# Two chained layers on one core: where the projection is added to the input, and where the second layer is prepared

## The chip, the core and the metric

The kernel runs on one core of a Trainium2 chip, all in float32. The metric is the device time of one execution in microseconds (us). The engines are PE (matrix multiply), DVE (vector), ACT (activations, scalar engine), POOL (GpSimd) and SP, which here only issues DMAs; ACT and POOL issue DMAs too, each engine in the order of its own queue. [...]

## What is computed

The input x is 384 channels of 192 x 192. Two layers follow each other, each added to its input:

```python
# layer 0
n = group_norm(x)                          # 32 groups of 12 channels
qkv = max_pool_2x2(w_qkv @ n + b_qkv)      # 1152 channels, 96 x 96
qkv = depthwise_3x3(qkv) + b_dw
q, k, v = split(qkv)                       # 8 heads of 48 channels
s = (q / |q|) @ (k / |k|).T * temperature  # 48 x 48 per head
out = sum(a_i * softmax(keep_top(s, k_i)) @ v for 4 sizes k_i)
x = x + repeat_2x2(w_proj @ gelu(out) + b_proj)
# layer 1
n = group_norm(x)
x = x + sum(bn_i(depthwise(n, w_i)) for 7 kernels)   # 13x13 and six smaller, dilated ones
```

The seven depthwise convolutions of layer 1 are folded into one 13 x 13 kernel per channel; the residual is put into its middle tap, as 1/scale of the group norm.

## The kernel before

**First statistics (lines 141 to 206).** x is loaded once, DVE takes bn_stats, and `group_stats` (109) turns channel statistics into scale and shift per channel (`gn0`) through small matmuls with the group matrix. The tap images' zero gaps are written to DRAM (`zd`).

**qkv stage (218 to 411).** 24 blocks of 8 input rows. A block has 18 steps (9 output groups of 128 channels, two halves): PE projects (`project`), DVE takes the 2x2 maximum out of PSUM (`pool`, line 280), ACT adds the bias, and one or two steps later DVE adds eight depthwise taps, four per step (`taps`, 316). PSUM holds two projections. Queries and keys are transposed and multiplied into a Gram matrix. ACT normalizes the next block's input in steps 9 to 14. The order is written out by hand: `at(step, f)` puts a piece of work ahead of a later step.

**Attention (414 to 529).** Ranks, softmax and the four masks become one block-diagonal matrix `bd`.

**Projection stage (532 to 594).** 24 blocks of 4 rows of 96. PE multiplies `bd` with v ("av", line 556), ACT applies Gelu, PE multiplies with w_proj ("pj", 567), ACT adds the bias (571), DVE adds the result to two rows of a fresh copy of x (577) and takes its statistics (581), POOL stores the sum to DRAM as `x1d`, rows of four interleaved (584).

**Layer 1, preparation (599 to 684).** From the statistics follow scale and shift (`group_stats`, `chp`); 1/scale goes into the middle tap; DVE spreads each channel's taps into 32 shifted images (`z`, 648), which are written to `zd`; matmuls make the tables `cb` (from `sv`) and `par` (from `rep`, "pp") and `edge`.

**Layer 1, convolution (686 to 816).** 48 tiles of 8 channels, and in a tile 8 x 5 matmuls with the tap images as weights. For each tile SP loads rows (`raw`, four transfers of 32 partitions, u = 0 to 3) and taps (`wt`, the same), ACT normalizes (726), DVE arranges into 16-column patches (741), PE multiplies (756), ACT evicts (764) out of four PSUM buffers, DVE turns the result back (770) and POOL stores it (779). Rows are loaded three tiles ahead, taps two, normalize runs two ahead, arrange one.

Of the kernel before, what the change touches and what calls it, by code (L numbers as in the profile page):

```python
# [45 lines left out]
PROW = MR * W  # L46
# [16 lines left out]
def tile_attn_then_large_kernel_conv(ctx: ExitStack, tc: tile.TileContext, a: dict, out: bass.AP):  # L63
# [7 lines left out]
    x1d = dram.tile([UQ * C * PROW + 2 * W], F32, name="x1d")  # L71
    zd = dram.tile([C * 32 * ZR * BC + 7 * BC], F32, name="zd")

    def x1_at(u, c, m):
        return x1d.offset + W + (u * C + c) * PROW + m * W
# [33 lines left out]
    def group_stats(pool, psum, mv, name):  # L109

        ps = psum.tile([NG, 1], F32, tag="gs", name=f"{name}_ps")
# [3 lines left out]
        nc.vector.tensor_copy(mean, ps)  # L115

        s = pool.tile([P, NJ, 1], F32, name=f"{name}_s")
        for j in range(NJ):
            pb = psum.tile([P, 1], F32, tag="gs", name=f"{name}_pb{j}")
            nc.tensor.matmul(pb, lhsT=gmt[:, j * P : (j + 1) * P], rhs=mean, start=True, stop=True)  # L120
            nc.vector.tensor_sub(s[:, j], mv[:, j, 0:1], pb)
            nc.vector.scalar_tensor_tensor(s[:, j], s[:, j], s[:, j], mv[:, j, 1:2], ALU.mult, ALU.add)
# [9 lines left out]
        return sb  # L132


    gn0 = const.tile([P, NJ, 2], F32, name="gn0")
    with (
# [57 lines left out]
        zero = s1.tile([1, W], F32, name="zero")  # L194
        nc.gpsimd.memset(zero, 0.0)
        for o in (0, W + UQ * C * PROW):
            nc.gpsimd.dma_start(out=bass.AP(x1d.tensor, x1d.offset + o, [[W, 1], [1, W]]), in_=zero)

        mv0 = s1.tile([P, NJ, 2], F32, name="mv0")
        for j in range(NJ):  # L200
            nc.vector.bn_aggr(mv0[:, j, :], stats[:, j].rearrange("p n s -> p (n s)"))
        sb0 = group_stats(s1, s_ps, mv0, "g0")
        for j in range(NJ):
            pb = s_ps.tile([P, 2], F32, tag="gs", name=f"g0_pc{j}")
            nc.tensor.matmul(pb, lhsT=gmt[:, j * P : (j + 1) * P], rhs=sb0, start=True, stop=True)
            nc.vector.tensor_copy(gn0[:, j, :], pb)  # L206


    mv1 = const.tile([P, NJ, 2], F32, name="mv1")
    with ExitStack() as ctx_v:  # L210
# [7 lines left out]
        with tc.tile_pool(name="gram", bufs=1, space=PSUM) as gps:  # L218
            gram = gps.tile([2 * CH, NPR, 2 * CH], F32, name="gram")
            with (  # L220
# [4 lines left out]
                tc.tile_pool(name="trps", bufs=2, space=PSUM) as trps,  # L225
            ):
# [35 lines left out]

                def project(b, m, sb):
# [14 lines left out]
                def pool(b, m, sb, ps):  # L278
                    mx = aw.tile([P, SR, WS], F32, tag="mx", name="mx", bufs=3)
# [45 lines left out]
                def end(b, m):  # L325

                    if m < 2 * NJ:
                        na = rows(b)[2]
                        junk = aw.tile([P, R + 1, WS], F32, name=f"junk_{b}_{m}", tag="junk")
                        nc.scalar.activation(  # L330
                            junk[:, :na], accs[b, m][:, :na], AF.Square, accum_out=ssq[:, m, b : b + 1]
                        )
# [49 lines left out]
                with tc.manual_schedule():  # L382
# [3 lines left out]
                    for sb in range(2):  # L386
                        for j in range(NJ):
                            normalize(0, sb, j)
                    for s in range(NB * NU):
# [8 lines left out]
                        if 9 <= u < 15 and b + 1 < NB:  # L398
                            normalize(b + 1, *divmod(u - 9, NJ))
                        if sb == 1:  # L400
# [14 lines left out]
            late_pool = ctx_v.enter_context(tc.tile_pool(name="late", bufs=1))  # L415
            bd = late_pool.tile([P, NJ, C], F32, name="bd")
            stats1 = late_pool.tile([P, NJ, HW // 512, 6], F32, name="stats1")
# [115 lines left out]
        NBK = RB * WS  # L533
        with (
            tc.tile_pool(name="b1", bufs=1) as b1,
            tc.tile_pool(name="bx", bufs=3) as bx,
            tc.tile_pool(name="bw", bufs=2) as bw,
            tc.tile_pool(name="b_ps", bufs=3, space=PSUM) as b_ps,
        ):
            wp = b1.tile([P, NJ, C], F32, name="wp")  # L540
            nc.sync.dma_start(out=wp, in_=a["wprojT"].rearrange("(j p) o -> p j o", p=P))
            bpj = b1.tile([P, NJ], F32, name="bpj")
            nc.sync.dma_start(out=bpj, in_=a["b_proj"])
            for b in range(HS // RB):
                r0 = 2 * b * RB
                xt = bx.tile([P, NJ, 2 * RB, W], F32, tag="xt", name=f"xb_{b}")
                nc.sync.dma_start(
                    out=xt.rearrange("p j r w -> p j (r w)"),
                    in_=x[:, r0 * W : (r0 + 2 * RB) * W].rearrange("(j p) n -> p j n", p=P),
                )  # L550
                g = bw.tile([P, NJ, NBK], F32, tag="g", name=f"g_{b}")
                for i in range(NJ):
                    ps = b_ps.tile([P, NBK], F32, tag="av", name="av")
                    js = AV_BLOCKS[i]
                    for j in js:
                        nc.tensor.matmul(
                            ps,
                            lhsT=bd[:, j, i * P : (i + 1) * P],
                            rhs=v[:, j, b * RB : (b + 1) * RB, :].rearrange("p r w -> p (r w)"),
                            start=(j == js[0]),  # L560
                            stop=(j == js[-1]),
                        )
                    nc.scalar.activation(g[:, i, :], ps, AF.Gelu)  # L563
                for i in range(NJ):
                    ps = b_ps.tile([P, NBK], F32, tag="pj", name="pj")
                    for j in range(NJ):
                        nc.tensor.matmul(  # L567
# [298 lines left out]
```

## Time and profile before

| | us |
|---|---|
| median of 3 runs (3372.46 to 3374.98) | 3374.6 |
| the profiled execution | 3371.7 |
| its span, first to last instruction | 3370.0 |
| PE busy | 2988.8 |
| DVE busy | 2572.3 |
| ACT busy | 1057.4 |
| POOL busy | 248.6 |

The profile is of one execution. A line of its groups of instructions gives source line, engine, operation, output<-inputs, shapes and count, then busy time, mean ns of one, and the idle time of the engine just before these instructions with what ended it. A float32 matmul of the program appears as two instructions. In rows by stretch of time each engine has its busy time, followed by PE's granted clock (1.00 is full), the share of time in which the 16 DMA engines were busy, and GB/s. The chain of waits goes back from the last instruction to what released each step. A DMA line gives the KB of one transfer and the median time from issue to landing.

### The profile page before, as it was taken

To read this page: it belongs to the slowest core of one execution; us is meant where nothing else is said; L and a number is where in the kernel's file an instruction comes from. 1 tells how busy PE (TensorE), PEld (TensorE's weight loads), DVE (VectorE), ACT (ScalarE), POOL (GpSimd) and SP (SyncE) were. 2 spreads that over 40 slices of the span, in tenths; PEclk is the share of its full clock that TensorE was granted. 3 is DMA by queue.
4 is the path that set the end of the run, shared out by engine and by line. 5 is a ranking of instruction groups with operands and counts; after the bars stand their busy time and mean duration, and the time that the engine had idled before them with its cause. 6 is when DMAs were issued, how large, how long until landed. Compare 5 with 4: busy or idle time off the path is not lost. (4 is left out here: it accounts for less than half of the span.)

```text
span 3370.0 us, 29135 instructions
## 1 busy us (share of the span) xinstructions
PE 2988.8 (89%) x10942; PEld 1981.1 (59%) x10942; DVE 2572.3 (76%) x3055; ACT 1057.4 (31%) x2114; POOL 248.6 (7%) x370
## 2 busy tenths in 40 slices
PE   0059999999999999999999956995399999999998
PEld 0036666666666666666666633553377777777776
DVE  5777888888888888888888898898477677676674
ACT  0013333333333333333333311221133333333332
POOL 2000000000000000000000001334011111111111
PEclk9999999999999999999999977998699999999999
DMA  9910011000001100000110005998999999999993
GB/s 400 425 75 28 29 46 39 28 29 28 29 29 45 40 28 29 29 29 28 45 41 29 0 13 217 400 410 338 228 232 210 208 208 210 207 209 208 207 209 90
DMA packets 144765, 449.14 MB, mean 133 GB/s; under 512 B 15824, under 2 KB 80320, under 8 KB 135312
## 3 DMA queue, kind: packets, MB, share of 16 engines
q1 hardware_dynamic: 106608, 293.20, 32.6%
q0 software_dynamic: 34592, 125.72, 11.9%
q10 hardware_dynamic: 3424, 28.37, 2.0%
q8 instruction: 86, 1.41, 0.2%
q14 instruction: 55, 0.45, 0.0%
HBM read 311.80 MB, written 135.42 MB: 133 GB/s over the span
## 5 line engine op out<-in xcount | busy, mean ns | idle before, releaser
L269 PE MATMUL qkv<-xt,wq 128*128 128x384 f32 x5184 | 1699.3, 487 | 0.5 <-ACT xt L261 0.5
L269 PEld LDWEIGHTS qkv<-xt,wq 128*128 128x128 f32 x5184 | 974.9, 190 | 650.8 <-ACT xt L261 1.3
L756 PE MATMUL conv<-xp,wt 128*128 128x288 f32 x3840 | 934.5, 407 | 44.7 <-DVE xp L741 44.7
L756 PEld LDWEIGHTS conv<-xp,wt 128*128 128x128 f32 x3840 | 731.3, 190 | 247.8 <-issue 44.9
L316 DVE SCALAR_TENSOR_TENSOR acc<-pooled,wd,acc 128x384 f32<-128x384 f32 (+2 forms) x1152 | 708.2, 615 | 30.6
L741 DVE STREAM_TRANSPOSE xp<-xn 128x384 f32<-128x384 f32 x96 | 440.5, 4588 | 313.3 <-PE conv L756 278.1
L280 DVE TENSOR_REDUCE mx<-qkv 128x192 f32<-128x768 f32 x432 | 413.7, 958 | 293.7 <-PE qkv L269 293.6
L287 ACT ACTIVATE pooled<-mx,bq 128x192 f32<-128x192 f32 x432 | 196.8, 456 | 1118.2 <-DVE mx L280 1118.2
L764 ACT ACTIVATE co<-conv,cb 128x288 f32<-128x288 f32 x384 | 191.4, 499 | 603.6 <-PE conv L756 603.6
L316 DVE SCALAR_TENSOR_TENSOR v<-pooled,wd,v 128x384 f32<-128x384 f32 (+2 forms) x576 | 354.0, 615 | 15.3
L770 DVE STREAM_TRANSPOSE o<-co 128x2304 f32<-128x2304 f32 x48 | 205.8, 4287 | 22.0 <-ACT co L764 22.0
L113 PE MATMUL g_ps<-mv,gm 128*32 128x1 f32 x12 | 1.6, 200 | 225.1 <-DVE bn_t L104 194.8
L779 POOL DMA_DIRECT2D out<-o x192 | 107.3, 593 | 903.6 <-DVE o L770 899.4
L149 DVE BATCH_NORM_STATS2 stats<-xs 128x6 f32<-128x512 f32 x216 | 128.8, 677 | 58.4 <-DMA xs<-in_x 58.4
L577 DVE TENSOR_TENSOR xb<-xb,pjs 128x768 f32<-128x768 f32 x144 | 132.1, 946 | 32.5 <-DMA xb<-in_x 27.5
L567 PE MATMUL pj<-g,wp 128*128 128x384 f32 x432 | 144.7, 489 | 12.9 <-ACT g L563 12.7
L261 ACT ACTIVATE xt<-xt,gn 128x768 f32<-128x768 f32 x144 | 145.3, 1012 | 2.0 <-DVE gn L206 2.0
L581 DVE BATCH_NORM_STATS2 stats<-xb 128x6 f32<-128x512 f32 x216 | 134.7, 678 | 0.0
L113 PEld LDWEIGHTS g_ps<-mv,gm 128*32 128x32 f32 x12 | 1.1, 140 | 226.0 <-DVE bn_t L104 194.8
L512 POOL MEMSET wide<- 96x1536 f32 x1 | 1.4, 1369 | 1782.2 <-issue 1782.2
L584 POOL DMA_DIRECT2D x1d<-xb x144 | 107.8, 753 | 242.5 <-DVE xb L577 242.5
L567 PEld LDWEIGHTS pj<-g,wp 128*128 128x128 f32 x432 | 80.9, 190 | 75.1 <-ACT g L563 21.5
(130 smaller groups left out, 1227.6 us busy)
## 6 DMA issues: line engine op xcount, KB each, us to landing
wt<-zd SPq DMA_DIRECT2D x192, 384.0 KB, 7.1
raw<-x1d SPq DMA_DIRECT2D x192, 312.0 KB, 11.5
xt<-in_x SPq DMA_DIRECT2D x48, 1152.0 KB, 5.5
xb<-in_x SPq DMA_DIRECT2D x24, 2304.0 KB, 13.2
x1d<-xb POOLq DMA_DIRECT2D x144, 384.0 KB, 7.7
out<-o POOLq DMA_DIRECT2D x192, 288.0 KB, 5.1
xs<-in_x ACTq DMA_DIRECT2D x12, 2304.0 KB, 14.7
xs<-in_x SPq DMA_DIRECT2D x12, 2304.0 KB, 24.3
```

The source lines that it names most:

```text
L261: nc.scalar.activation(xt[:, j], xt[:, j], AF.Identity, bias=gn0[:, j, 1:2], scale=gn0[:, j, 0:1])
L269: nc.tensor.matmul(ps[:, r, : 2 * W], lhsT=wq[:, j, m * P : (m + 1) * P], rhs=xt[:, j, r * 2 * W : (r + 1) * 2 * W], start=(j == 0), stop= ...
L280: nc.vector.tensor_reduce(mx, ps[:, :, : 2 * W].rearrange("p r (y w x) -> p r w y x", y=2, x=2), AX.XY, ALU.max,)
L287: nc.scalar.activation(pool_t[m][:, k : k + SR, 1 : 1 + WS], mx, AF.Identity, bias=bq[:, m : m + 1])
L316: nc.vector.scalar_tensor_tensor(acc[:, :nt], pool_t[m][:, k0 + dy : k0 + dy + nt, dx : dx + WS], wd[:, m, t : t + 1], acc[:, :nt], ALU.mu ...
L567: nc.tensor.matmul(ps, lhsT=wp[:, j, i * P : (i + 1) * P], rhs=g[:, j, :], start=(j == 0), stop=(j == NJ - 1))
L577: nc.vector.tensor_add(xv, xv, up)
L581: nc.vector.bn_stats(stats1[:, i, b * nst + n, :], xf[:, n * 512 : (n + 1) * 512])
L741: nc.vector.transpose(bass.AP(at.tensor, at.offset, [list(at.ap[0]), [NBQ, n], [1, NBQ], [NQ * NBQ, CC], [ME * NBQ, NE]],), bass.AP(row.te ...
L756: nc.tensor.matmul(ps, lhsT=wt[:, c, o : o + P], rhs=d[:, c, g : g + 2 * NT - 1 : 2, :], start=(g == 0), stop=(g == NGR - 1),)
L764: nc.scalar.activation(co[:, c], ps, AF.Identity, bias=cb[:, cc : cc + 1])
L770: nc.vector.transpose(bass.AP(at.tensor, at.offset, [list(at.ap[0]), [2 * W, TE], [BC, NBQ], [W, 2], [1, BC]]), bass.AP(of.tensor, of.offs ...
```

## The change

- `x1d` is gone. The projection stage becomes two passes. Pass one makes av and Gelu for all blocks, with Gelu written in place over v. Pass two has the output groups of 128 channels outermost and 24 blocks in each; its results are stored to DRAM as `pds`, even and odd rows apart, without being added to x.
- In the qkv stage POOL makes 2x2 sums of the normalized input and stores them to DRAM (`sums`). The second layer's statistics are put together from those sums (mean, and covariance with the projection through a "cell" of sum/4 + projection), and from the first statistics.
- The derivation of scale, shift, taps and tables runs three times, after each output group, as a generator `derive` that is advanced once per block of pass two, and once per channel of the convolution; the tap images are spread in quarters by POOL through one buffer. An 8-channel tile that shares a group with the next 128 channels is left to the next round.
- In the convolution stage rows of x and of the projection are loaded apart, and POOL adds them (`residual`). Transfers for u = 0, 1 are issued by SP, those for u = 2, 3 by ACT. The first tile is prepared during pass two. In the qkv stage `junk` goes to PSUM and `mx` has 2 buffers instead of 3. The zero rows of `x1d` are no longer written.

In the diff below ZQ is 8 (four pieces of `z` per round), KK is 16, NBB is 24, `group_stats` has six yields, `patches` is two memsets on POOL, the matmuls of `sv` are called "shp" in the profile, `load_sum` prefetches four blocks, and the part of pass two that is left out is three pj matmuls, ACT's bias to `pj` and SP's store of `pj` to `pds[i]`. Its core, with the parts that the prediction uses:

```diff
-    x1d = dram.tile([UQ * C * PROW + 2 * W], F32, name="x1d")
+    sums = dram.tile([C, HS * WS], F32, name="sums")
+    pds = [dram.tile([2, P, HS // 2 * WS], F32, name=f"pd{j}") for j in range(NJ)]
...
+                def add_up(b, sb, j):
+                    xv = xts[b, sb][:, j].rearrange("p (r y w x) -> p r y w x", r=SR, y=2, x=2)
+                    t = aw.tile([P, SR, WS], F32, tag="sum", name="sum", bufs=2)
+                    nc.gpsimd.tensor_add(t, xv[:, :, 0, :, 0], xv[:, :, 0, :, 1])
+                    nc.gpsimd.tensor_add(t, t, xv[:, :, 1, :, 0])
+                    nc.gpsimd.tensor_add(t, t, xv[:, :, 1, :, 1])
+                    nc.gpsimd.dma_start(
...
...
                         if 9 <= u < 15 and b + 1 < NB:
                             normalize(b + 1, *divmod(u - 9, NJ))
+                            at(s + 1, add_up, b + 1, *divmod(u - 9, NJ))
...
+        def place(j, p0, p1):
+            for c0 in range(0, 32, ZQ):
+                z = d1.tile([P, ZQ, K0 * BC], F32, name="z", tag="z")
+                nc.gpsimd.tensor_copy(
+                    z.rearrange("p a (r x) -> p a r x", x=BC),
...
+                )
+                nc.sync.dma_start(
...
+                    in_=z[p0:p1],
+                )
+                yield
+        def derive(i, stats):
+            nc.vector.bn_aggr(mvt, stats[:, i].rearrange("p n s -> p (n s)"))
+            nc.vector.tensor_add(mv1[:, i], mvt, pre[:, i])
+            yield
+            yield
+            pc = yield from group_stats(d1, d_ps, mv1, f"g1_{i}")
...
+            yield
+            if i > 0:
+                yield from place(i - 1, P - CC, P)
+            yield from place(i, 0, P if i == NJ - 1 else P - CC)
+            for j in range(max(0, i - 1), i + 1):
+                nc.gpsimd.tensor_copy(sv, mean[:, j : j + 1].to_broadcast([P, P]))
+                yield
+                yield
+                nc.tensor.matmul(ps, lhsT=sv, rhs=ident, start=True, stop=True)
+                nc.vector.tensor_copy(cb[:, j * P : (j + 1) * P], ps)
+                yield
+            for k in range(KK):
+                r = d1.tile([P, UQ, CC, NE], F32, name="rep", tag="rep", bufs=4)
...
+                if k % 4 == 3:
+                    yield
+                    for q in range(k - 3, k + 1):
+                        nc.tensor.matmul(
+                            pp[:, q],
...
...
+        def queue(u):
+            return nc.sync if u < 2 else nc.scalar
...
+        def residual(k):
+            rv = raws[k].rearrange("p m (w x) -> p (m w) x", x=2)
+            uv = ups[k].rearrange("p m w -> p (m w)").unsqueeze(2).to_broadcast([P, (ME + 1) * WS, 2])
+            nc.gpsimd.tensor_add(rv, rv, uv)
...
+                for n in range(NJ * NBB):
+                    i, b = divmod(n, NBB)
+                    load_sum(n + 4)
+                    if b == 0 and i > 0:
+                        running.append(derive(i - 1, stats1))
+                    advance()
...
+                    nc.vector.scalar_tensor_tensor(t, smj.pop(n), quarter[:, i : i + 1], ps, ALU.mult, ALU.add)
+                    nc.vector.bn_stats(stats1[:, i, b, :], t)
...
+                    if n == NBB + 4:
+                        both(load_rows, 0)
+                    if n == NBB + 12:
+                        residual(0)
+                    if n == 2 * NBB:
+                        both(load_taps, 0)
+                        for q in range(3):
+                            normalize1(0, q)
+                    if n == 2 * NBB + 4:
+                        running.append(arrange(0, 2))
+                while running:
+                    advance()
+                running.append(derive(NJ - 1, stats1))
+                advance()
...
+            both(load_rows, 1)
+            both(load_taps, 1)
+            patches(l2, 1)
+            residual(1)
+            both(load_rows, 2)
+            for q in range(3):
+                normalize1(1, q)
+            for k in range(NK):
+                load_rows(k + 3, (0, 1))
+                load_taps(k + 2, (0, 1))
+                residual(k + 2)
+                for c in range(CC):
+                    convolve(k, c, co)
+                    advance()
+                    if c == 0:
+                        load_rows(k + 3, (2, 3))
+                        load_taps(k + 2, (2, 3))
...
+                    if 3 <= c < 6 and k + 2 < NK:
+                        normalize1(k + 2, c - 3)
```

## What was predicted

> **What bounds the kernel now.** I read the busy times by stage first, because the shares of the whole span average over stages with different limits, then the chain of waits, then groups of instructions with their shapes. Columns of the first view: stretch and length in us, busy time and instructions of PE, PE's weight loads, DVE, ACT and POOL, granted clock, DMA share, GB/s.
> ```profile
> 211.00:1987.00 1776.00, 1770.63 (x6201) 1077.92 (x6200) 1440.30 (x2160) 647.55 (x1429) 0.00 (x0) 1.00 0.09 30
> 1987.00:2056.00 69.00, 7.85 (x38) 7.60 (x39) 63.44 (x76) 1.85 (x3) 1.37 (x1) 0.50 0.06 16
> 2056.00:2352.00 296.00, 255.25 (x780) 146.92 (x779) 262.25 (x367) 73.51 (x145) 120.62 (x148) 0.95 0.98 385
> 2352.00:2421.00 69.00, 12.79 (x57) 11.88 (x58) 34.55 (x45) 4.51 (x5) 0.00 (x0) 0.50 0.83 224
> 2421.00:3355.00 934.00, 933.96 (x3840) 730.89 (x3839) 625.67 (x141) 323.08 (x524) 105.04 (x188) 1.00 0.93 202
> ```
> The reader is to see: PE without a gap in the qkv stage (first row) and in the convolution (last row); the projection stage (2056 to 2352) with DVE, PE and DMA all nearly full; then 69 us in which PE has 13 us of work.
> ```profile
> 2360.86 6.42 DVE z L648
> 2367.28 0.02 issue
> 2367.30 12.05 DMA zd<-z
> ...
> 2385.81 13.97 DMA zd<-z
> ...
> 2412.16 8.21 DVE xp L741
> 2420.36 0.30 issue
> 2420.67 17.60 PE conv L756 x60
> 2438.27 0.04 issue
> 2438.31 916.93 PE conv L756 x3780
> ```
> This is the chain (start, length): statistics, tap images, their writes, first load and arrange, in series, and then PE to the end. Its first 60 matmuls took 17.60 us where 916.93/3780 makes 14.6: 3 us for the clock, 0.50 in the gap.
> ```profile
> L567 PE MATMUL pj<-g,wp 128*128 128x384 f32 x432 | 144.7, 489 | 12.9 <-ACT g L563 12.7
> L581 DVE BATCH_NORM_STATS2 stats<-xb 128x6 f32<-128x512 f32 x216 | 134.7, 678 | 0.0
> L577 DVE TENSOR_TENSOR xb<-xb,pjs 128x768 f32<-128x768 f32 x144 | 132.1, 946 | 32.5 <-DMA xb<-in_x 27.5 <-DMA x1d<-xb 2.8 <-ACT pjs L571 2.1
> L556 PE MATMUL av<-v,bd 128*128 128x384 f32 x336 | 114.0, 492 | 0.7 <-DVE bd L529 0.7
> ```
> In the projection stage DVE carries 134.7 + 132.1 us and waits 32.5: it is the bound, with DMA close behind. PE alone would need 258.7 us.
>
> **The change, part by part**, against the profiled execution (3371.7 us, span 3370.0, 2.9 under the median of 3374.6).
>
> *Projection in two passes, no add, no x1d.* From the first av matmul (2057.8) to the first convolution matmul (2420.67) lie 363 us. The 144 DVE adds, 216 statistics, 144 stores and the whole gap leave this path. What stays is PE: 114.0 us (av), then 144.7 us (pj). Beside them lie, in pass one, 72 Gelus at 0.49 us and 72 statistics of 384 elements (about 0.54 by the 512-element row), 35 and 39 us under 114; in pass two, per block of 2.0 us, ACT 0.58 and DVE 0.62 (the 384-element row of L316) + 0.54. So PE bounds both. Between them wp (4.0 us to landing) goes where bd lay, so it can only be issued after the last av matmul: +5 (0 if it were placed elsewhere). 363 - 264: **-99**. The regrouped first statistics save the hops of two copies and three pairs: **-1**.
>
> *Derive, three times.* PE: some 58 small matmuls; pp's 32 took 7.0 us at clock 0.50, so 3.5 at full; with the others 5.3 each: **+16**. The rest is put on POOL and SP beside PE, with PE's own next step in a fixed place of its queue, and there it can wait. One piece of z is a quarter: copy 6.42/4 = 1.6 us if POOL is as fast as DVE (memset row on POOL: 4896 elements in 4.2 us, so 1.4 at least; for a read and a write, 2.9; I take 1.6, the row of the same copy). Its write: 2 us of latency, as the smallest loads here, and a quarter of the other 10: 4.5. z has one buffer, so a piece takes 6.1, and one of 8 partitions 1.6 + 2.2 = 3.8; PE allows 2.0 per piece. Behind the waiting SP write stand the next sum load and pd store; behind POOL's copy, sv, for which PE waits.
> - Output block 0: three pieces at 6.1, a copy of 1.6, then the residual of tile 0, queued ahead of sv (2496 elements: 2.1 us at the memset rate, 6.4 in three passes; I take two, 4.3): 24 us against the 6 blocks (12 us) that PE has in between: **+12**.
> - Output block 1: four small and four large pieces, 35 us, against 10 blocks: **+15**. Its last steps no longer fit beside pass two: three rounds of four 512-element copies (0.5 each) that PE waits for, with the hops: **+7**.
> - Then two memsets (2.4 + 4.2), residual 1 and normalize 1 (3.2) stand ahead of ACT's first eviction, 18 us after POOL is free, against four PSUM banks (9.7 us) and that tail: **+4**.
> - Output block 2, in the convolution's second tile (block time 19.45): POOL's second piece is queued behind four stores that wait for DVE (9.2 + 4.3 us), so it starts 16.3 us in; pieces to 47.6, residual 4 to 52, the first normalize to 54. ACT stands at that normalize, behind it the evictions; PE stops after four banks at 39: **+15**.
> - After three such stops the clock may ramp again, 3 us each as above, once already in before: **+6** (0 to 9).
>
> *Convolution.* PE's 934.6 us are unchanged. DVE is as before (13.5 of 19.45). POOL adds the residual (4.3) to four stores (2.4); ACT gets six DMA issues (0.45 each on SP in before, 2.7 us) beside 7.2 us of work. All under 19.45, and four banks ride over the issues. DMA is the narrow one.
> ```profile
> wt<-zd SPq DMA_DIRECT2D x192, 384.0 KB, 7.1
> raw<-x1d SPq DMA_DIRECT2D x192, 312.0 KB, 11.5
> ...
> out<-o POOLq DMA_DIRECT2D x192, 288.0 KB, 5.1
> ```
> A tile moves 4 x (384 + 312 + 288) KB, the change adds 4 x 156 for the projection rows: 4.03 to 4.67 MB, 240 GB/s. It also cuts raw into rows of 768 bytes. In the trace's packet records, wt's 1536 bytes take 65 ns where a transfer spans all partitions (wp's load), but 124 on average here, where each spans 32. While SP's queue passes from partitions 32-63 to 64-95 the rate rises from 195 to 258 GB/s. Loads for partitions 0-63 on one queue and 64-127 on the other make this mixture lasting, so I take 260 GB/s or more: 3.49 MB in 13.4 us, stores 4.7, sum 18.1 under 19.45: **0**. Below it bounds (rival B).
>
> [...]
>
> *2x2 sums in the qkv stage.* 432 POOL adds of 192 elements (0.17 us at the memset rate, 0.5 in three passes; I take 0.35, DVE's row for 192 elements) and 144 stores (0.75 each). POOL did nothing here. PE bounds the stage; a DVE step is reduce 0.96, four taps 2.57, idle 0.42. **0** as long as POOL leaves DVE alone; no row shows both reading SBUF together. Bounds: 0 to +70 (rival C). mx on two buffers costs nothing: ACT empties one 0.46 us after its reduce.
>
> [...]
>
> Sum: -99 - 1 + 16 + 12 + 15 + 7 + 4 + 15 + 6 = -25: 3346.7, or on the footing of the median **3350 us**. With single terms off, 3320 to 3385. Chance 0.46, of which 0.34 is faster by over 0.2% (about what a measurement of this kernel can tell from no change), 0.08 within, 0.04 slower.
>
> **Rivals.**
> - *A, the chains keep up* (0.18, faster): POOL and SP run ahead of PE because writes of quarter images overlap or POOL copies faster. Without the three stops and their clock, -48: 3302. For it: DMA is nearly idle in pass two. Against: one z buffer makes copy and landing strictly serial.
> - *B, the DMA engines bound the convolution* (0.14, slower): two queues don't add up. Place: every tile; it decides when loads run under 237 GB/s, (3.49 MB in 19.45 - 4.7 us). At the stage's 202 it is 17.3 + 4.7 = 22.0, +2.5 x 46 tiles: 3465. For it: DMA already 0.93 full here. Against: the rise at each change of half.
> - *C, POOL takes DVE's read port in the qkv stage* (0.12, slower): three adds of 0.5 a step against 0.42 idle; over six steps DVE falls back 6.5 us, one PSUM buffer rides over 3; 3 us x 23 blocks: 3420. It decides where an add costs over some 0.3 us and cannot run under the reduce.
> - *D, POOL at its upper prices* (0.10, half of it within 0.2%, half slower): copies of 2.9, residual of 6.4, some +34 over the three chains: 3384.
>
> That the work doesn't leave DVE at all is excluded: no add and a quarter of the statistics remain there.
>
> **How the numbers follow.** Faster 0.34 + 0.18 = 0.52; within 0.08 + 0.05 = 0.13; slower 0.04 + 0.14 + 0.12 + 0.05 = 0.35. The range takes in C and most of A and leaves out B's upper part: 3295 to 3440.
>
> **What would show it.** PE of av and pj near 259 us with DVE half idle; pj's stretch near 195 us with stops at shp; in the convolution's third tile one stop of some 15 us that ends with POOL's residual; elsewhere no PE gap; DMA share under 0.95 with wt packets under 100 ns. PE gaps in every tile, released by loads, are B; idle PE in the qkv stage released by DVE's reduce, with longer taps in six steps of 18, is C. The forecast is wrong if POOL's pieces follow each other much faster or slower than 6 us, or if an order of queues that I read from the code is not the built one.

## Result and profile after

The changed kernel takes **3478.9 us** (median of 4 runs, 3474.7 to 3483.3), the kernel before 3374.0 in the same session: ratio 1.031, 95% interval 1.029 to 1.033. The prediction said 3350, 3295 to 3440. Its direction and its range were wrong. The profiled execution took 3474.7 us with a span of 3472.9, so 128 us more than the 3346.7 that the prediction has for this footing.

First the stages, in the view of busy times by stretch (columns as in the prediction).
```profile
208.00:1988.00 1780.00, 1774.21 (x6206) 1079.72 (x6206) 1459.84 (x2161) 651.51 (x1433) 377.58 (x577) 1.00 0.12 38
2062.00:2176.00 114.00, 110.01 (x336) 64.47 (x336) 39.01 (x88) 36.58 (x73) 0.00 (x0) 0.98 0.46 147
2176.00:2412.00 236.00, 170.91 (x555) 101.83 (x556) 102.85 (x197) 45.80 (x78) 54.30 (x44) 0.84 0.59 162
2412.00:2437.00 25.00, 12.39 (x47) 9.98 (x48) 12.01 (x8) 3.41 (x4) 15.04 (x8) 0.64 1.09 248
2437.00:2546.00 109.00, 64.33 (x272) 49.86 (x272) 48.11 (x28) 21.27 (x36) 49.31 (x34) 0.80 0.73 169
2546.00:3455.00 909.00, 878.15 (x3571) 677.17 (x3572) 579.28 (x134) 285.03 (x485) 309.16 (x227) 0.99 1.01 218
```
Rows one and two went as forecast: qkv and pass one are full of PE work. (1780 us against 1776 before is the choice of stretch. From the first qkv matmul to the last one of the Gram matrix both kernels take 1776.7 us.) From row three on PE has holes: 78 us in the 261 of rows three and four, 45 in the next 109, 31 in the 909 after. In the last row 3 of the 31 are the end of one wait of the derivation; the other 27 are lost a little at a time, 1.9 us at most, where before had none (933.96 of 934.00).

The first pj matmul, in the timeline of PE:
```profile
2176.16 14.25 PE L918 MATMUL pj<-v,wp 128*128 128x384 f32 x36 [4.02 <-DMA wp<-in_wprojT]
```
The prediction's terms up to here give 2175.8 (2057.8 - 1 + 114.0 + 5). So nearly all of the 128 us were lost behind this point. From here to the convolution's first long run, at 2437.3, PE's chain takes 261 us. Without the 12.6 us of 40 convolution instructions in it that is 249, against some 197 by the terms (144.7 of pj, 10.7 of matmuls, 12 + 15 + 7 + 4, and 4 of clock): +51. From there to the end it takes 1048 us with those 12.6, against 972 (934.6 and 14.7 for the convolution and the end behind it, 5.3, 15 and 2): +77.

The groups that answer to those of before:
```profile
L918 PE MATMUL pj<-v,wp 128*128 128x384 f32 x432 | 156.2, 521 | 9.9 <-DVE cell L933 5.9 <-DMA wp<-in_wprojT 4.0
L586 PE MATMUL av<-v,bd 128*128 128x384 f32 x336 | 110.0, 491 | 0.7 <-DVE bd L555 0.7
L933 DVE SCALAR_TENSOR_TENSOR cell<-smj,quarter,pj 128x384 f32<-128x384 f32 x72 | 43.7, 607 | 172.0 <-ACT pjs L926 154.3 <-DMA smj<-sums 15.7 <-DMA pd<-pjs 1.4
L934 DVE BATCH_NORM_STATS2 stats_t<-cell 128x6 f32<-128x384 f32 x72 | 40.4, 560 | 2.5
```
DVE's 266.8 us of adds and statistics are down to 84.1 here, with 35.5 more in pass one, and it waits. The pj matmuls cost 11.5 us more than before. The granted clock is 0.84 and 0.64 in the rows with the stops; in v1 below, which has no such stops, it is 0.98 and pj takes 147.1.

Who waits for what (us in total, times, longest), from the table of waits:
```profile
ACT co L854 <- DMA raw<-in_x: 194.5, 20, 11.5
ACT co L854 <- DMA up<-pd: 164.2, 19, 10.1
PE shp L708 <- POOL sv L704: 95.4, 3, 42.2
ACT pjs L926 <- DMA pd<-pjs: 87.9, 17, 9.0
```
The third line is three stops of 26, 27 and 42 us, where the prediction had 12, 15 and 15. The others it did not have. In the first two lines, ACT's evictions of the convolution wait for a load they do not use, some 9 us in 39 tiles. One such tile, in the timelines of ACT and PE:
```profile
2975.18 0.32 ACTq L774 DMA_DIRECT2D raw<-in_x  x1
2975.60 0.43 ACTq L781 DMA_DIRECT2D up<-pd  x1
2976.07 0.43 ACTq L774 DMA_DIRECT2D raw<-in_x  x1
2976.54 0.48 ACTq L781 DMA_DIRECT2D up<-pd  x1
2978.14 7.02 ACTq L795 DMA_DIRECT2D wt<-zd  x2
2985.20 1.28 ACT L854 ACTIVATE co<-conv,cb 128x288 f32<-128x288 f32 x3 [9.53 <-DMA raw<-in_x]
```
```profile
2985.76 4.63 PE L846 MATMUL conv<-xp,wt 128*128 128x288 f32 x18 [0.92 <-ACT co L854]
```
ACT passes four issues in 2 us, then stands before the last two. Three evictions queue up behind them, PE runs the four buffers that take its results in PSUM full and stops for 0.92 us. Idle time of ACT that ends with a DMA, ahead of an instruction that reads none: the thing to look for is in its queue, not in its operands.

The first stop, in POOL's timeline and then PE's:
```profile
2259.47 3.30 POOL L661 COPY z<-wf 128x1664 f32<-128x1664 f32 x1 [8.30 <-DMA zd<-z]
2269.03 3.29 POOL L661 COPY z<-wf 128x1664 f32<-128x1664 f32 x1 [6.25 <-DMA zd<-z]
2278.55 3.29 POOL L661 COPY z<-wf 128x1664 f32<-128x1664 f32 x1 [6.23 <-DMA zd<-z]
2281.81 4.89 POOL L808 TENSOR_TENSOR raw<-raw,up 128x2496 f32<-128x2496 f32 x1
2286.65 0.29 POOL L704 COPY sv<-mean 128x128 f32<-128x128 f32 x1
```
```profile
2286.99 0.79 PE L708 MATMUL shp<-ident,sv 128*128 128x128 f32 x2 [25.99 <-POOL sv L704]
```
The order is the predicted one: three pieces, a copy, the residual, then sv, and PE behind it. The sizes are not: a piece takes 9.5 us (copy 3.3, landing 6.2), against 6.1 predicted. The third round's pieces take 7.4, as they land in 4.1 us. The first two rounds write 120 partitions, the third 128; so it is in e1_all_sp (below) too, issue to landing:
```profile
zd<-z SPq DMA_DIRECT2D x8, 780.0 KB, 6.1
zd<-z SPq DMA_DIRECT2D x4, 832.0 KB, 4.0
```
No run changes the number of partitions alone, so that it is the cause is not shown. The third stop lies in the convolution's third tile:
```profile
2519.13 0.80 PE L708 MATMUL shp<-ident,sv 128*128 128x128 f32 x2 [42.21 <-POOL sv L704]
```
The prediction had PE stop there behind ACT, whose evictions wait behind a normalize that waits for the residual. But PE stands for sv itself, which POOL has behind eight pieces and the residual.

### The profile page after: what moved, and what is told of

It reads as the page before. It is cut to its first block, busy times and chain, and to the rows that moved or that the text cites. A ratio compares the mean times of both kernels' runs of the same rounds, so it can differ in the third digit from the quotient of the medians.

```text
span 3472.9 us, 30852 instructions
## 1 busy us (share of the span) xinstructions
PE 3025.5 (87%) x11058; PEld 1996.5 (57%) x11058; DVE 2455.7 (71%) x2955; ACT 1048.8 (30%) x2116; POOL 834.0 (24%) x922
## 4 chain that ended last, share of the span: by engine, by line
PE 74%; DMA 15%; DVE 6%; POOL 2%; issue 1%; ACT 1%; ACTq 0%; SPq 0%; POOLq 0%; DVEq 0%
PE qkv L294 48%; PE conv L846 17%; DMA up<-pd 5%; DMA raw<-in_x 4%; PE av L586 3%; DMA xs<-in_x 3%; PE pj L918 3%; DVE stats L166 2%; DMA zd<-z 2%; POOL z L661 1%; PE gram L382 1%; PE tr L370 1%; ACT co L854 1%; DMA wt<-zd 0%; DVE xp L830 0%
## 5 line engine op out<-in xcount | busy, mean ns | idle before, releaser
L846 PE MATMUL conv<-xp,wt 128*128 128x288 f32 x3840 | 951.5, 410 | 27.4 <-ACT co L854 26.9
L341 DVE SCALAR_TENSOR_TENSOR acc<-pooled,wd,acc 128x384 f32<-128x384 f32 (+2 forms) x1152 | 724.2, 629 | 30.6
L830 DVE STREAM_TRANSPOSE xp<-xn 128x4608 f32<-128x4608 f32 (+2 forms) x101 | 440.0, 4357 | 320.2 <-PE conv L846 306.7
L854 ACT ACTIVATE co<-conv,cb 128x288 f32<-128x288 f32 x384 | 183.4, 500 | 723.4 <-PE conv L846 345.9
L280 POOL TENSOR_TENSOR sum<-xt 128x192 f32<-128x192 f32 x144 | 98.2, 682 | 1245.3 <-ACT xt L274 1245.1
L341 DVE SCALAR_TENSOR_TENSOR v<-pooled,wd,v 128x384 f32<-128x384 f32 (+2 forms) x576 | 357.7, 621 | 15.3
L808 POOL TENSOR_TENSOR raw<-raw,up 128x2496 f32<-128x2496 f32 x48 | 240.6, 5012 | 16.5 <-DMA raw<-in_x 10.3
L933 DVE SCALAR_TENSOR_TENSOR cell<-smj,quarter,pj 128x384 f32<-128x384 f32 x72 | 43.7, 607 | 172.0 <-ACT pjs L926 154.3
L918 PE MATMUL pj<-v,wp 128*128 128x384 f32 x432 | 156.2, 521 | 9.9 <-DVE cell L933 5.9
L661 POOL COPY z<-wf 128x1664 f32<-128x1664 f32 x20 | 66.1, 3307 | 301.8 <-DVE mean L696 189.1
L918 PEld LDWEIGHTS pj<-v,wp 128*128 128x128 f32 x432 | 86.1, 203 | 70.2 <-issue 14.6
```

Of the source, the lines that this page charges most:

```text
L341: nc.vector.scalar_tensor_tensor(acc[:, :nt], pool_t[m][:, k0 + dy : k0 + dy + nt, dx : dx + WS], wd[:, m, t : t + 1], acc[:, :nt], ALU.mu ...
L808: nc.gpsimd.tensor_add(rv, rv, uv)
L830: nc.vector.transpose(bass.AP(at.tensor, at.offset, [list(at.ap[0]), [NBQ, n], [1, NBQ], [NQ * NBQ, CC], [ME * NBQ, NE]],), bass.AP(row.te ...
L846: nc.tensor.matmul(ps, lhsT=wt[:, c, o : o + P], rhs=d[:, c, g : g + 2 * NT - 1 : 2, :], start=(g == 0), stop=(g == NGR - 1),)
L854: nc.scalar.activation(co[:, c], ps, AF.Identity, bias=cb[:, cc : cc + 1])
L918: nc.tensor.matmul(ps, lhsT=wp[:, j, i * P : (i + 1) * P], rhs=v[:, j, b * RB : (b + 1) * RB, :].rearrange("p r w -> p (r w)"), start=(j = ...
```

## Experiments

All but the last are single executions with a profile; the differences that verdicts rest on are read in the stages. The changed kernel took 3474.7 to 3483.3 us, median 3478.9.

**The steady loss: two queues or ACT's queue.** Theory M: the mixture of two queues carries the rate, so one queue would be much slower. Theory W: the DMA engines are full, so that moving issues gains nothing. Theory Q: ACT's evictions wait behind its own DMA issues.

*e1_all_sp*, all loads on SP:
```diff
-            return nc.sync if u < 2 else nc.scalar
+            return nc.sync
```


> The changed kernel with every load of the convolution issued by SP; ACT issues none. In the changed kernel's steady convolution (2546 to 3455 us) PE stands 31 us of 909 and ACT is stopped some 9 us per tile at its own DMA issues. Theory Q (ACT's queue is the cause: its evictions stand behind DMA issues that wait for earlier transfers): those PE gaps close, 25 to 45 us less in all, about 3440. Theory W (the DMA engines are full, 4.67 MB a tile at some 230 GB/s): no gain, the waits move to the arrival of rows and taps. Theory M (the mixture of both partition halves on two queues carries the rate, as I had predicted): with one queue the loads fall to 195 GB/s, 17.9 us and 4.7 of stores, 22 us a tile, over 100 us more, about 3590.

Measured: 3445.7 us, -33. *e2_spread* keeps ACT's issues, spread over the tile:
```diff
+                    if c in (0, 2) and k + 3 < NK:
+                        load_rows(k + 3, (2 + c // 2,))
+                    if c in (4, 6) and k + 2 < NK:
+                        load_taps(k + 2, (c // 2,))
                     if c == 0:
-                        if k + 3 < NK:
-                            load_rows(k + 3, (2, 3))
-                        if k + 2 < NK:
-                            load_taps(k + 2, (2, 3))
```


> The changed kernel with ACT's six DMA issues of a tile spread over the evictions of channels 0, 2, 4 and 6 instead of all behind channel 0. Theory Q (ACT's queue): a transfer has drained before the next issue stands at the head of the queue, PE gaps of the steady convolution (31 us) shrink to under 10, about 3450. Theory W (DMA engines full): unchanged within 10 us, the gaps only move.

Measured: 3441.4 us. The stretch 2546 to 3410 of the changed kernel, of e1_all_sp and of e2_spread:
```profile
2546.00:3410.00 864.00, 833.15 (x3385) 641.93 (x3386) 559.76 (x130) 273.81 (x464) 302.46 (x215) 0.99 1.05 226
```
```profile
2546.00:3410.00 864.00, 858.12 (x3543) 672.58 (x3542) 584.00 (x135) 296.67 (x481) 311.20 (x228) 1.00 1.04 232
```
```profile
2546.00:3410.00 864.00, 858.13 (x3528) 672.00 (x3527) 585.85 (x134) 297.13 (x481) 307.50 (x225) 0.99 1.00 230
```
PE's idle time falls from 30.9 us to 5.9 in both, and those 5.9 are one wait of the derivation. One has a single queue, at 232 GB/s, so M falls; the DMA share stays full and PE gains all the same, so W falls too. Q stands. PE also executes some 140 to 160 instructions more in the same time: its matmuls got shorter with the stops gone (951.5 us in all in the changed kernel, 944.4 in e2_spread).

*b1_split*: the kernel before, with its own loads split over SP (u = 0, 1) and ACT (u = 2, 3).
```diff
-                    nc.sync.dma_start(
+                    (nc.sync if u < 2 else nc.scalar).dma_start(
```


> The kernel before with only the convolution's loads split over two queues (partitions 0-63 by SP, 64-127 by ACT behind channel 0), same bytes and same packets. Before: DMA share 0.93, a wt packet of 1536 bytes takes 124 ns on average. Theory M (the halves mix and the ports add up): packets fall towards 65 to 90 ns, DMA share under 0.75, time within 0.2% of before. Against it: share and packet times stay within 10%, time within 0.2% if ACT's issues don't block (rows of 9984 bytes make few descriptors), some 30 us more if they do.

Measured: 3382.7 us beside 3374.5. The loads are not faster: in 2546 to 3330 the DMA moves 206 GB/s at a share of 0.96, 202 at 0.94 in before; a 1536-byte packet takes 120 ns on SP's queue and 133 on ACT's, 124 in before. The 8 us lie ahead of the convolution's first matmul, for which PE waits 54.1 us (44.7 before), as ACT does 60.0 us for the layer's first rows (50.6 before); in the stretch named PE works 784.00 of 784 us, as in before, so that the GB/s there are PE's pace. And ACT's four issues pass without a wait:
```profile
2941.74 0.79 ACTq L699 DMA_DIRECT2D raw<-x1d  x2
2942.65 0.86 ACTq L713 DMA_DIRECT2D wt<-zd  x2
```

**What makes the issue wait.** Three theories: the number of transfers open on ACT (N), the pieces they are cut into (P), the bytes (R). *e7_up_sp* moves up to SP:
```diff
-                queue(u).dma_start(
+                nc.sync.dma_start(
                     out=up[u * 32 : (u + 1) * 32].rearrange("p m w -> p (m w)"),
```


> The changed kernel with the projection rows (up) of all four u issued by SP; ACT keeps four transfers per tile, two of raw (32 x 13 rows of 768 bytes each, 416 pieces) and two of wt (256 pieces of 1536 bytes each). Theory N (an engine may have only so many transfers open before its next issue waits; in the changed kernel the fifth and sixth waited 7.0 us): four issues pass in 2 us, ACT is free, the time falls to about 3445. Theory P (the wait comes with the pieces a transfer is cut into; 1344 remain here of 1408): the fourth issue still waits some 5 us or more and the time stays within 10 of 3475. Theory R (it comes with the bytes that are open: 1392 KB here, 1704 in the changed kernel, 1392 in b1_split without a wait): no wait, as N.

Measured: 3447.3 us; ACT's last two issues take 2.4 to 2.5 us, a wait of some 1.6. P falls. *b2_six* takes b1_split and cuts each of ACT's two wt transfers in two:
```diff
-                for u in us:
+                for u, h in [(u, h) for u in us for h in range(1 if u < 2 else 2)]:
+                    n = CC if u < 2 else CC // 2
...
-                        out=wt[u * 32 : (u + 1) * 32],
+                        out=wt[u * 32 : (u + 1) * 32, h * n : (h + 1) * n],
```


> The kernel before with its loads split over SP and ACT as in b1_split (3382.7 us, four ACT issues in 1.65 us), and each of ACT's two wt transfers cut in two by channels: six transfers per tile on ACT, with the same bytes and the same pieces (about 580). Theory N (number of open transfers): the fifth and sixth issue wait several us as in the changed kernel, ACT evicts late and the time rises by 15 or more, to 3398 and over. Theory P (pieces) and theory R (bytes): no wait, some 1 us more of issuing beside idle time of ACT, 3380 to 3388.

Measured: 3396.2 us, and the wait is there, with the same bytes and pieces as b1_split. It makes PE stop seven times, 5.0 us in all (778.74 of the 784 us worked); 12 us lie ahead of the convolution, as 9 do in b1_split.
```profile
2932.09 0.79 ACTq L699 DMA_DIRECT2D raw<-x1d  x2
2932.98 7.90 ACTq L714 DMA_DIRECT2D wt<-zd  x4
2940.93 0.50 ACT L766 ACTIVATE co<-conv,cb 128x288 f32<-128x288 f32 x1 [8.34 <-DMA raw<-x1d]
```
R falls too. N looked right, but before itself has eight transfers per tile on SP, issued in 3.7 us without a wait. The traces offer another reason, theory S: SP's and ACT's transfers share eight counters, given out in turn in the program's order; each raises its counter when it lands, and waits for that counter before it is issued, so each waits for the landing of the transfer eight before it.

The traces show the counters as numbered semaphores. In before, where SP issues every load of the convolution, a transfer waits for, and raises, the counter of the eighth before it in all 295 cases between 2560 and 3300 us. In the changed kernel, between 2560 and 3400 us, all 492 loads (244 of SP, 248 of ACT) wait for the counter that they raise; both engines use the same eight, each 61 or 62 times, as turns of eight would have it, and POOL's stores use eight others. ACT's six in the tile shown above:
```
issued   what  counter  raised last by      landed
2975.18  raw   112      SP's raw, 2954.22   2961.20
2975.60  up    114      SP's up, 2954.71    2961.95
2976.07  raw   115      ACT's wt, 2957.53   2968.74
2976.54  up    107      SP's up, 2963.80    2970.97
2978.14  wt    111      SP's wt, 2972.74    2978.12
2984.85  wt    114      ACT's up, 2975.60   2984.82
```
In 39 tiles of this stretch the sixth goes out 0.02 us behind the landing of an up that ACT itself had issued 7.9 to 10.2 us before. (The table of waits names raw for about half of these; by its counter it is up in all 39.)

Two runs put six transfers on ACT with only eight per tile on both engines. *b3_six_of_eight* is b1_split with u = 1, 2, 3 on ACT:
```diff
-                    (nc.sync if u < 2 else nc.scalar).dma_start(
+                    (nc.sync if u < 1 else nc.scalar).dma_start(
```


> The kernel before with its eight transfers per tile split two on SP and six on ACT (u = 1, 2, 3). Theory S: the built program has eight counters for the landings of SP's and ACT's transfers together, given out in turn, and a transfer waits for the landing of the one eight before it; with eight per tile that one belongs to the tile before and has long landed. So ACT issues all six in some 3 us without a wait, and the time is that of b1_split, 3380 to 3390. Theory N (ACT may have some four transfers open): the fifth and sixth wait 6 to 8 us as in b2_six, and the time is 3395 or more.

Measured: 3390.4 us; in 2546 to 3330 PE works 784.00 of 784. *e9_up_pool* does it in the changed kernel, with up on POOL's queue:
```diff
-            return nc.sync if u < 2 else nc.scalar
+            return nc.sync if u < 1 else nc.scalar
...
-                queue(u).dma_start(
+                nc.gpsimd.dma_start(
                     out=up[u * 32 : (u + 1) * 32].rearrange("p m w -> p (m w)"),
```


> The changed kernel with the projection rows (up) issued by POOL, whose transfers have other counters, and raw and wt split two on SP and six on ACT, so that SP and ACT together have eight per tile instead of twelve. Theory S: ACT's six pass without a wait, no eviction is late for a transfer in the even tiles, PE is full from 2546 on (858 of 864 us as in e1_all_sp and e2_spread), and the time is 3440 to 3455. Theory N: six on ACT wait as in the changed kernel, some 9 us per tile, and the time stays at 3465 to 3490.

Measured: 3442.3 us, PE 858.4 of the 864. ACT's issues in b3_six_of_eight, then in e9_up_pool:
```profile
2929.85 3.01 ACTq L699 DMA_DIRECT2D raw<-x1d  x3
2932.95 1.39 ACTq L713 DMA_DIRECT2D wt<-zd  x3
```
```profile
2923.59 1.37 ACTq L774 DMA_DIRECT2D raw<-in_x  x3
2925.06 1.45 ACTq L795 DMA_DIRECT2D wt<-zd  x3
```
Six pass in 2.9 to 4.4 us, without the 7 us. N falls and S holds. But the number per tile is not all: e7_up_sp has twelve too, and PE loses nothing there (858.1 of the 864). The next table has what ACT's last two issues wait for. For the changed kernel it is what the trace shows; for the others it follows from S and the order of transfers in the program. Beside it stand the idle times of ACT ahead of an eviction that end with the landing of a load (us in all, times, longest; the issues' own time is in them).

| run | transfers per tile, SP and ACT | ACT's last two issues wait for | ACT's wt issues take | ACT's waits that end with a load |
|---|---|---|---|---|
| changed | 12 | SP's wt, ACT's own up, of the same turn | 7.0 us | 361.3, 40, 11.5 |
| b2_six | 10 | SP's wt, ACT's own raw, of the same turn | 7.9 us (four) | 347.4, 42, 10.0 |
| e7_up_sp | 12 | SP's up, SP's wt | 2.4 to 2.5 us | 108.6, 37, 5.7 |
| b3_six_of_eight | 8 | the same transfers, of the turn before | 1.4 us (three) | 151.6, 38, 5.0 |
| e9_up_pool | 8 | the same transfers, of the turn before | 1.4 to 2.1 us (three) | 121.2, 37, 7.6 |

A turn is one pass of the loop over tiles. The long waits are those for a transfer that ACT itself issued shortly before, as the changed kernel's chain of waits shows:
```profile
2914.75 9.25 DMA up<-pd
2924.00 0.02 issue
2924.02 0.31 ACTq L795
2924.33 0.05 issue
2924.38 0.51 ACT co L854
```

**The stops of the derivation.** *e3_slow_derive* advances it in the convolution once per tile and not once per channel:
```diff
                     convolve(k, c, co)
-                    advance()
+                    if c == 6:
+                        advance()
```


> The changed kernel with the third derivation advanced once per tile of the convolution instead of once per channel (its tables are not needed before tile 29). In the changed kernel PE stands 42 us in the second tile for sv, which is queued on POOL behind seven pieces of z, and 109 us at the start of the convolution hold only 64 us of PE. Theory P (the pieces of z, at 7 to 10 us each, arrive faster than POOL and SP can work them off): the 42 us stop goes, 35 to 50 us less, about 3435. Theory W (DMA is full there and the stop hides a transfer that is late anyway): under 15 us less.

Measured: 3423.6 us, -55. The third stop is gone (PE's waits for sv: 53.1 us in two), and PE works 99.8 us of the 109 after 2437, not 64.3. The steady loss stays (836.9 of 864).

Which queue makes PE wait? *e4_sv_dve* takes sv and rep off POOL, *e5_z_pool* takes the writes of z off SP, *e6_both* does both.
```diff
-                nc.gpsimd.tensor_copy(sv, mean[:, j : j + 1].to_broadcast([P, P]))
+                nc.vector.tensor_copy(sv, mean[:, j : j + 1].to_broadcast([P, P]))
...
-                nc.sync.dma_start(
+                nc.gpsimd.dma_start(
                     out=bass.AP(
                         zd.tensor,
```


> The changed kernel with the copies for sv and rep on DVE instead of POOL, so that no matmul of PE waits for something queued on POOL behind pieces of z. In the changed kernel PE waits 27, 28 and 42 us for sv in the three rounds. Theory POOL (PE's fixed step stands behind POOL's pieces, as predicted): 40 to 60 us less in pass two and its tail, about 3430. Theory SP (each block of pass two also puts one write of z on SP's queue, ahead of the pd store that ACT waits for, so pass two runs at the pace of the pieces, 6 to 10 us a block, whoever makes sv): under 20 us less in pass two; the third stop stays too, because POOL's residual stands behind the pieces.

> The changed kernel with the writes of z issued by POOL itself instead of SP, so that sum loads, pd stores and the convolution's loads no longer stand behind them; sv stays on POOL. Theory SP: pass two's blocks no longer run at the pace of the pieces, ACT's waits for pd stores (88 us in sum) go. Theory POOL: PE still waits for sv behind the pieces, so no more than 15 us are won in all, about 3465.

> Both at once: sv and rep on DVE, z written by POOL. If both queues hold PE back in parallel (each alone wins little), this wins much more than the sum of the two single edits: pass two from 236 us to 170 to 190, some 50 us less, about 3425; the stop in the convolution's second tile (residual behind the pieces) stays, some 30 to 40 us. If the pieces were not the cause at all, nothing changes.

Measured: 3470.0, 3496.2 and 3441.2 us: -9, +17 and -38 (against 3478.9). In e4_sv_dve PE's waits for sv fall from 95.4 to 15.3 us, but ACT still waits 99.0 us for stores of pd, which SP issues in turn with the writes of z. In e5_z_pool those fall to 19.3, but sv still waits for POOL's pieces, 113.7. Either queue alone holds PE at the pace of the pieces; only both together free it. Adding the single effects would have given +8. In SP's queue it is the order, as the changed kernel's timeline shows: a store of pd goes out 0.4 us behind a write of z, which waited for POOL's copy, and ACT stands until that store lands.
```profile
2366.13 0.50 SPq L936 DMA_DIRECT2D pd<-pjs  x1
2371.91 3.29 POOL L661 COPY z<-wf 128x1664 f32<-128x1664 f32 x1 [6.24 <-DMA zd<-z]
2372.43 0.58 ACT L926 ACTIVATE pjs<-pj,bpj 128x384 f32<-128x384 f32 x1 [8.95 <-DMA pd<-pjs]
2375.23 0.34 SPq L669 DMA_DIRECT2D zd<-z  x1
2375.66 0.50 SPq L936 DMA_DIRECT2D pd<-pjs  x1
```
In e6_both a third stop remains, and now by the route that was predicted: PE waits 41.5 us for one eviction, and ACT up to 49.1 us for POOL's residual.

**The sums in the qkv stage.** *e8_one_add* makes one add of three (the second statistics then come from half of each cell):
```diff
                     nc.gpsimd.tensor_add(t, xv[:, :, 0, :, 0], xv[:, :, 0, :, 1])
-                    nc.gpsimd.tensor_add(t, t, xv[:, :, 1, :, 0])
-                    nc.gpsimd.tensor_add(t, t, xv[:, :, 1, :, 1])
```


> The changed kernel with only the first of the three adds of the 2x2 sums, so the second statistics come from half of each cell; everything is still stored. It prices POOL's work beside the qkv stage, which took 1780 us for 1776 before. If POOL's reads slow DVE and DVE holds PE (rival C), the stage falls back to some 1777 us; if the sums are hidden and the 4 us come from elsewhere, it stays at 1779 to 1781. DVE's taps, 629 ns a piece on the mean in the changed kernel and 615 before, should fall to about 620 where the two share a port. The whole time stays within 6 us of 3475 either way.

Measured: 3474.6 us, the same stretch with PE at 1774.4 (1774.2 in the changed kernel, 1773.6 in before), the taps (128 x 384 into acc) at 629 ns (630, and 616 in before). 199 us less of POOL's work change nothing, so two of the adds cost nothing. The stage has no 4 us to explain: from its first qkv matmul to the last one of the Gram matrix it takes 1776.9 us here and 1776.7 in the other two.

**A version without the waits.** *v1*: all loads on SP; sv and rep on DVE; z written by POOL; the second and third derivation spread over the rest of pass two and the first 29 tiles of the convolution; the first tile's rows and taps loaded one transfer per block, the second tile's normalize and arrange moved behind the first tile's first evictions.
```diff
+            steps = [1] * 5 + [2] * 4 + [3] + [2] * 5 + [1] * 8 + [2] * 6
...
                     convolve(k, c, co)
-                    advance()
+                    if k == 10 and c == 0:
+                        running.append(derive(NJ - 1, stats1))
+                    if k < len(steps) and c in (6, 2, 7)[: steps[k]]:
+                        advance()
...
-                    if n == NBB + 4:
-                        both(load_rows, 0)
+                    if NBB + 2 <= n < NBB + 6:
+                        load_rows(0, (n - NBB - 2,))
```


> All that the traces point to at once: all loads on SP; sv and rep on DVE; z written by POOL; the second and third derivation spread over the convolution's first 29 tiles, one or two steps a tile, instead of one per block or channel; tile 0's rows and taps loaded one transfer per block of pass two; tile 1's normalize behind tile 0's first evictions. If the stops are the queues' order and nothing else, what is left is 110 us of av, 145 to 165 of pass two, some 15 at the start of the convolution, 935 and 12 us of PE for the derivations: 3300 to 3330. If the DMA engines are short in the convolution once nothing else delays it, its tiles take over 19.5 us and the time stays above 3345.

Measured: 3318.6 us. The same kernel, timed:

> The kernel of v1 again, now timed for an interval. One look gave 3318.59 us beside 3371.95 for the kernel before. If that was the kernel and not the execution, the median lies between 3312 and 3325 us and the ratio to the kernel before between 0.981 and 0.986.

Measured: **3319.9 us** (5 runs, 3318.5 to 3320.1) beside 3374.8: ratio 0.984, interval 0.982 to 0.985. Pass two, the start of the convolution and the rest of it:
```profile
2176.00:2340.00 164.00, 157.31 (x529) 92.74 (x530) 106.64 (x211) 46.13 (x78) 34.44 (x16) 0.98 0.73 208
2340.00:2460.00 120.00, 101.35 (x404) 78.42 (x403) 67.60 (x18) 36.99 (x59) 65.08 (x34) 0.91 1.08 243
2460.00:3300.00 840.00, 840.00 (x3517) 659.33 (x3516) 575.30 (x192) 285.82 (x466) 331.35 (x230) 1.00 1.03 236
```
PE has no gap in the last 840 us, though the DMA share is full. All loads are on SP here, twelve transfers per tile: SP's issues wait for counters too (before's trace, above), but SP evicts nothing. What is left are 18.6 us in two stops at the convolution's start.

## Why the prediction was wrong, point by point

- **The projection in two passes, -99, and the -1: right in sum, in part by luck.** The first pj matmul came at 2176.2, by the terms at 2175.8. But av began 4.3 us late, at 2062.1, and took 110.0 us, not 114.0; wp took 4.0, not 5. Of the 4.3 us, 0.7 are the first statistics, where -1 was expected. The rest lies ahead of `bd`: DVE's eight small copies into `wide` took 6.81 us (1.32 before), the longest 4.24, while POOL ran two memsets of 2.35 and 4.30 us that before does not have there. The times fit; no run takes the two apart.
- **Three stops, where they are: right; their sizes: wrong, a step that failed.** The terms +12, +15 and +15 measured 26, 27 and 42. The piece was mis-sized: 6.1 us predicted, 9.5 measured in the first two rounds and 7.4 in the third. The strided copy on POOL takes 3.3 us (DVE's row was taken, 1.6; the "upper price" of 2.9 was nearer). The landing takes 6.2 us for 120 partitions; the 4.5 taken fits the 128 of the third round (4.1). The residual was 5.0, not 4.3. The third stop also came by another route, sv and not the evictions.
- **One step missing: ACT waits for pd's stores on SP.** The prediction named this queue ("behind the waiting SP write stand the next sum load and pd store") and priced only sv. e4_sv_dve, e5_z_pool and e6_both together show that it holds PE by itself. Rival D, POOL at its upper prices, had nearly the right copy (2.9 for 3.3) and with 34 us too little: it left out the landing, SP and ACT's queue.
- **"Four banks ride over the issues", 0: the step that failed in the convolution.** Six issues of 0.45 us were priced. The last two take 7 us, as one waits for the landing of a transfer that ACT issued 7.9 to 10.2 us before (the changed kernel's trace, and b2_six against b3_six_of_eight). Its cost is 27 us of late evictions, which are gone in e1_all_sp, e2_spread, e7_up_sp and e9_up_pool, and some 8 of slower matmuls.
- **"The mixture" of two queues, 260 GB/s or more: not seen, and it did not matter.** Its signs were a DMA share under 0.95 and wt packets under 100 ns; the share is 1.05 and the packets take 120 ns on SP's queue and 126 on ACT's. (The 65 ns of wp's load are a median; their mean is 77.) Rival B falls all the same: PE is full in v1, on one queue. The rows' 230 to 236 GB/s are loads and stores together at PE's pace, so they can't be held against B's 237 for loads alone. What a second queue adds no run measures, as PE is full in before and in b1_split; the packets got no shorter there (120 and 133 ns for 124).
- **The sums, 0, and rival C: right to give it little.** POOL's adds took 0.60 to 0.78 us where 0.35 was taken, the taps went from 616 to 630 ns, and PE lost nothing (1776.7 us in both kernels). The read port that C has POOL take from DVE was an assumption, and no run shows it: four taps took 2.57 us before and 2.69 in the steps with adds of over 2 us in all.

Together: of the +51 in pass two and its tail, 26 are the two stops for sv, 8 the slower pj matmuls (11.5, 4 predicted), 8 the small matmuls (18.7, 10.7 predicted), 6 the stop at the convolution's start (9.86 us measured, 4 predicted) and 6 waits for cell. That makes 54; the records of matmuls that follow each other overlap by some 4 us. Of the +77 in the convolution 27 are the third stop, 27 the late evictions, 15 the slower matmuls (951.5 us for 934.6, 2 predicted), 6 a wait for rep in the third derivation and 2 its small matmuls.

## What to carry to other kernels

Before a load is given to an engine that also computes, find out which landing its issue must wait for. Here it is that of the transfer eight before, counted over SP and ACT, which share the eight counters: with eight per turn of the loop ACT's six issues passed in 2.9 to 4.4 us, with the changed kernel's twelve the last one stood 5.8 to 8.0 us for an up that ACT had issued 7.9 to 10.2 us before. It is not the issue's own time that counts, but that wait, and who stands behind it in the queue. When a chain is moved beside other work, price every queue it goes through: freeing one of two queues that run at the same pace gained little or nothing here (-9 and +17 us, both together -38). A chain that has time should be given the time: stepping it once per tile took the third stop away, and 55 us with it.

## What was not expected of the hardware

- A strided copy on POOL takes 3307 ns for 1664 elements per partition, 2.0 ns an element, as does its two-input add (5012 ns for 2496), while small adds of 192 elements take 0.60 to 0.78 us, 3.1 to 4.1 ns an element.
- Loads that each span 32 partitions kept PE as full from one queue (858.12 of 864 us, e1_all_sp) as from two (858.13, e2_spread), at a full DMA share.
- A write of 780 KB from 120 partitions landed in 6.1 us, one of 832 KB from 128 partitions in 4.0 (e1_all_sp); the packets are of 832 bytes in both, and in the changed kernel they took 53 to 61 ns in the first and 40 to 51 in the second. Beside the full convolution (e3_slow_derive, v1) the second took 8.1 to 10.0 us.
